# Sharing the tail chunk of two batches' keys, and making all 1601st keys in one product

## The chip, the core and the metric

The kernel runs on one core of a Trainium2 chip. Times are device microseconds of one launch. TensorE is called PE here (PEld its weight loads), VectorE DVE, ScalarE ACT, GpSimd POOL; SP is the queue that issues nearly all transfers.

## What is computed

A small transformer of three layers runs on x, of 16 batches x 64 rows x 256. What matters here is the first layer's cross-attention: each batch has its own context of 1601 rows x 256. From it come 8 heads of 128 keys each, every key is layer-normalised over its 128 numbers, and two query heads attend to each key head. Cut to that:

```python
kvx = jnp.einsum('bsi,oi->bso', cond, w_kv_x)          # cond: (16, 1601, 256)
kx, vx = jnp.split(kvx, 2, axis=-1)
kx = _ln(kx.reshape(b, sc, g, d), kxln_w, kxln_b)      # g = 8 heads, d = 128
xout = _gqa(qx, kx, vx).reshape(b, s, nh * d)          # softmax(qx kx / sqrt(d)) vx
```

Self-attention with 8-bit weights stands beside it in that layer, and its output and xout are rounded and projected together. A block attention with a feed-forward and a second feed-forward follow; they touch the change only by sharing the engines.

## The kernel before

**Tiles.** The 16 batches are taken two at a time, which gives 8 tiles (index i) of 128 query rows. The 8 key heads are taken in two halves of 4 (index hh)[...]. A batch (bb, 0 or 1 within its tile) and a half make a *unit*, and the two units of one tile and half make a *pair*; there are 32 units and 16 pairs. The 1601 keys of a unit are cut into NC = 13 chunks, 12 of 128 and a last one, the tail, of 65 (`TAIL`).

**One chunk's way**, all in `unit`:
- `load_T` (L471) fetches two chunks of the transposed context at once into `ctxT` (4 buffers); the tail is fetched alone, as 65 columns;
- `project` (L484) multiplies by the half's key weights `wkx`: two matmuls (L488) into one of two PSUM buffers of the pool `ps_mm`; ACT squares the result (L493). The weights have their mean over each head taken out beforehand by `centre`, so that normalising needs the squares only;
- `squares` (L496): DVE sums the squares per head (L499), POOL makes the inverse root in `rsqrt` (L159, L160);
- `normalise` (L504): DVE multiplies (L507), which frees the PSUM buffer;
- `transpose_k` (L517): PE transposes the four heads (L521), ACT applies the normalisation's weight and bias while copying out (L523), giving `kT`;
- `score` (L529): PE multiplies keys and queries (L534), ACT copies the scores to a tile P of the pool `pp` (L539), and DVE keeps a running maximum (L544);
- `exponent` (L583): once the unit's maximum is known, DVE subtracts it (L585) and ACT takes the exponential (L589);
- `accumulate` (L591): PE multiplies P and the plain context `ctxN` (L604) into three PSUM banks, over all chunks of the unit.

After the tail the sums are divided, transposed, and in `pair_out` (L655) multiplied with the value weights for both batches of the pair.

**Order.** Nothing loops at run time. `at(step, rank, fn)` and `spawn(step, rank, generator)` put work into a heap, and `run` emits it by step, then by rank. A unit's chunk c is projected in step base + c, scored in base + c + 2, exponentiated in base + c + 18 and accumulated in base + c + 20; its context is asked for in base + c - 5. The units' bases are 13 steps apart, so each step carries one chunk of each of these stages, 416 steps in all, with the other layers' work spread between them. The layer below then lays out each engine's instruction stream in nearly this order; two calls of `behind` hold back some DVE instructions. A tile of a pool is given to a new user when all the readers of its former user are done. `pp` has 19 buffers of 512 columns.

```python
at(base + c, 2, lambda c=c: project(c))
at(base + c, 4.2, lambda c=c: squares(c))
at(base + c + 1, 1, lambda c=c: normalise(c))
at(base + c + 1, 6, lambda c=c: transpose_k(c))
at(base + c + 2, 5, lambda c=c: score(c))
```

The first half of `wkx` is loaded at the very start and centred in step -6, the second is loaded in step 6 and centred at the end of step 9. `more_constants` asks for the constants that are needed later, in step -1, all on SP's queue.

Of the kernel before, what the change touches and what calls it, by code (L numbers as in the profile page):

```python
# [14 lines left out]
F32 = mybir.dt.float32  # L15
# [3 lines left out]
AF = mybir.ActivationFunctionType  # L19
ALU = mybir.AluOpType  # L20
AX = mybir.AxisListType
PSUM = bass.MemoryType.PSUM

P = 128
B, S, H = 16, 64, 256
T = 1601
NH, G, D = 16, 8, 128
NT = B * S // P
NP = 4
NC = (T + P - 1) // P  # L30
TAIL = T - (NC - 1) * P
EPS = 1e-5
FP8_MAX = 448.0
INTER = 704
# [24 lines left out]
def body(tc, ctx, a):  # L59
    nc = tc.nc  # L60
    V, A, PE, GP = nc.vector, nc.scalar, nc.tensor, nc.gpsimd

    const = ctx.enter_context(tc.tile_pool(name="const", bufs=1))
    small = ctx.enter_context(tc.tile_pool(name="small", bufs=8))
    wp = ctx.enter_context(tc.tile_pool(name="wp", bufs=10))
    ctxp = ctx.enter_context(tc.tile_pool(name="ctxp", bufs=4))
    kp = ctx.enter_context(tc.tile_pool(name="kp", bufs=3))
    pp = ctx.enter_context(tc.tile_pool(name="pp", bufs=19))
    qp = ctx.enter_context(tc.tile_pool(name="qp", bufs=2))
    one = ctx.enter_context(tc.tile_pool(name="one", bufs=1))  # L70
    dram = ctx.enter_context(tc.tile_pool(name="dram", bufs=2, space=bass.MemoryType.DRAM))
    ps_mm = ctx.enter_context(tc.tile_pool(name="ps_mm", bufs=2, space=PSUM))
# [3 lines left out]
    def tr_tile(name, dt=F32):  # L76
        return ps_s.tile([P, 512], dt, tag="s", name=name)

    def s_tile(name):
        return ps_s.tile([P, 512], F32, tag="s", name=name)  # L80
# [4 lines left out]
    def spawn(step, rank, gen):  # L85
        heapq.heappush(heap, (step, rank, next(count), gen))

    def at(step, rank, fn):
        def once():
            fn()  # L90
            yield 1

        spawn(step, rank, once())
# [16 lines left out]
    wkx = const.tile([P, 2, 1024], F32, tag="wkx", name="wkx")  # L110

    def col(name, j=0):
        s = _COLS[name].start + j
        return vec[:, s : s + 1]

    ident = const.tile([P, P], F32, tag="ident", name="ident")
# [28 lines left out]
    def more_constants():  # L145
        for i in range(1, NT):
            nc.sync.dma_start(out=xr[i], in_=xs_in[i])
        nc.sync.dma_start(out=rows, in_=a["rows"].partition_broadcast(P))
        nc.sync.dma_start(out=shp, in_=a["shapes"])


    def rsqrt(out, in_, scale, g):

        n = in_.shape[0]
        ve = small.tile([P, 8], F32, tag="ve", name="ve")
        if scale is None:
            GP.tensor_scalar(ve[:n, :g], in_, EPS, None, ALU.add)
        else:
            GP.tensor_scalar(ve[:n, :g], in_, scale, EPS, ALU.mult, ALU.add)  # L159
        GP.tensor_tensor(out, ve[:n, :g], nhalf[:n, :g], ALU.pow)  # L160
# [49 lines left out]
    def v2(t):  # L210
        return t.rearrange("p (k o) -> p k o", k=2)
# [109 lines left out]
    def project(out, xq, ws, o, n):  # L321
        for k in range(2):
            for e, w in enumerate(ws):
                PE.matmul(  # L324
                    out, lhsT=xq[:, k, :], rhs=v2(w)[:, k, o : o + n],
                    start=k + e == 0, stop=k == 1 and e == len(ws) - 1,
                )
# [125 lines left out]
    def rows_of(c):  # L453
        return P if c < NC - 1 else TAIL

    pairs, mark = {}, {}

    def behind(ins, other):

        tc.add_manual_dep(  # L460
            ins.ins, other.ins.name,
            mybir.DependencyInfo(mybir.DependencyClass.NoSync, mybir.DependencyReason.DATA), reason="order",
        )

    def unit(i, hh, bb, base):
        b = 2 * i + bb
        last = b == B - 1 and hh == 1
        st = {"cxT": {}, "cxN": {}, "ps": {}, "ss": {}, "rs": {}, "kn": {}, "kT": {}, "P": {}, "pT": {}}
        pair = pairs.setdefault((i, hh), {})

        def load_T(c):  # L471
            t0 = c * P
            n = min(256, T - t0)
            t = ctxp.tile([P, 2, 256], F32, tag="ctxT", name="ctxT")
            nc.sync.dma_start(out=t[:, :, :n], in_=a["ctx"][b].rearrange("(k p) t -> p k t", p=P)[:, :, t0 : t0 + n])
            st["cxT"][c // 2] = t

        def load_N(c):
            n = rows_of(c)
            t = next(ctxn_next)  # L480
            nc.sync.dma_start(out=t[:n, 0:H], in_=a["ctx_n"][b][c * P : c * P + n, :])
            st["cxN"][c] = t

        def project(c):  # L484
            n, o = rows_of(c), (c % 2) * P
            ps = ps_mm.tile([P, 512], F32, tag="mm", name="ps_k")
            for k in range(2):
                PE.matmul(  # L488
                    ps[:n, :], lhsT=st["cxT"][c // 2][:, k, o : o + n], rhs=wkx[:, k, 512 * hh : 512 * (hh + 1)],
                    start=k == 0, stop=k == 1,  # L490
                )
            sq = one.tile([P, 512], F32, tag="sq", name="sq")
            A.activation(sq[:n], ps[:n], AF.Square)  # L493
            st["ps"][c], st["ss"][c] = ps, sq

        def squares(c):  # L496
            n = rows_of(c)
            ss = small.tile([P, 4], F32, tag="ss", name="ss")
            mark["ss"] = V.reduce_sum(ss[:n], st["ss"].pop(c)[:n].rearrange("p (g d) -> p g d", g=4), axis=AX.X)  # L499
            rs = small.tile([P, 4], F32, tag="rsx", name="rsx")  # L500
            rsqrt(rs[:n], ss[:n], 1.0 / D, 4)
            st["rs"][c] = rs

        def normalise(c):  # L504
            n, ps, rs = rows_of(c), st["ps"].pop(c), st["rs"].pop(c)
            kn = one.tile([P, 512], F32, tag="kn", name="kn", bufs=2)
            mark["kn"] = V.tensor_tensor(  # L507
                kn[:n].rearrange("p (g d) -> p g d", g=4), ps[:n].rearrange("p (g d) -> p g d", g=4),
                rs[:n].unsqueeze(2).to_broadcast([n, 4, D]), ALU.mult,
            )  # L510

            for name in ("M", "mx"):
                if name in mark:
                    behind(mark["kn"], mark[name])
            st["kn"][c] = kn

        def transpose_k(c):  # L517
            n, kn = rows_of(c), st["kn"].pop(c)
            tr = tr_tile("tr_kx")
            for g in range(4):  # L520
                PE.transpose(tr[:, g * P : g * P + n], kn[:n, g * D : (g + 1) * D], ident[:n, :n])  # L521
            kT = kp.tile([P, 4, P], F32, tag="kT", name="kT")
            A.activation(  # L523
                kT[:, :, 0:n], tr.rearrange("p (g t) -> p g t", g=4)[:, :, 0:n],
                AF.Identity, bias=col("kxln_b"), scale=col("kxln_w"),
            )
            st["kT"][c] = kT

        def score(c):  # L529

            n, kT = rows_of(c), st["kT"].pop(c)
            ps = s_tile("s")
            for g in range(4):
                PE.matmul(  # L534
                    ps[:n, g * P : (g + 1) * P], lhsT=kT[:, g, 0:n],
                    rhs=qxs[i, hh][:, bb, 2 * g : 2 * g + 2, :].rearrange("p h s -> p (h s)"), start=True, stop=True,
                )
            pc = pp.tile([P, 512], F32, tag="P", name="P")
            A.activation(pc[:n], ps[:n], AF.Copy, scale=C_ATT)  # L539
            if c == 0:  # L540
                st["M"] = one.tile([P, 512], F32, tag="M", name="M")
                mark["M"] = V.tensor_copy(st["M"], ps)
            else:
                mark["M"] = V.tensor_tensor(st["M"][:n], ps[:n], st["M"][:n], ALU.max)  # L544
            st["P"][c] = pc
# [82 lines left out]
            A.copy(pair["pc"][:, k, :, bb, :], tr.rearrange("p (g q) -> p g q", g=4))  # L628

        for c in range(NC):  # L630
            if c % 2 == 0:
                at(base + c - 5, 0, lambda c=c: load_T(c))
            at(base + c, 2, lambda c=c: project(c))
            at(base + c, 4.2, lambda c=c: squares(c))
            at(base + c + 1, 1, lambda c=c: normalise(c))
            at(base + c + 1, 6, lambda c=c: transpose_k(c))
            at(base + c + 2, 5, lambda c=c: score(c))
            at(base + c + 17, 0, lambda c=c: load_N(c))
            at(base + c + 18, 8, lambda c=c: exponent(c))
            at(base + c + 20, 3.5, lambda c=c: accumulate(c))  # L640
# [401 lines left out]
    at(6, 0, lambda: load_wkx(1))  # L1042
    at(9, 9, lambda: centre(1))
    at(-1, 0, more_constants)
    EX = 4.0
    for i in range(NT):
        base = 52 * i
# [6 lines left out]
        )  # L1054
        spawn(ln0, EX, ln_tile(i))
        for p in range(4):
            spawn(sa0[p] - 2, EX, self_attention(i, p))
            spawn(qx0[p] - 2, EX, queries(i, p))
        l0 = base + {NT - 3: 96, NT - 2: 80, NT - 1: 74}.get(i, 92)
# [79 lines left out]
```

## Time and profile before

| | us |
|---|---|
| median of 3 runs | 2729.69 |
| lowest, highest | 2727.47, 2730.16 |
| the profiled execution's own time | 2729.8 |
| its span, first to last instruction | 2728.0 |
| busy: PE, PEld | 2616.5, 2022.0 |
| busy: DVE, ACT, POOL | 1892.1, 1410.4, 847.3 |

The mean granted PE clock was 0.985. The profile is of one execution. A group of instructions is one line of the kernel, one engine, one shape; in a timeline its columns are start, length, engine, line, operation, output and inputs, and in square brackets the idle time before it with what ended it. For matmuls the first pair of numbers (128*65) is the stationary operand, 65 being the number of keys, and what follows (128x512) the streamed one. Every fp32 matmul of the program shows as two instructions, so that a chunk's product, two matmuls, is a group of x4; a transpose is one.

### The profile page before, as it was taken

What the parts mean: (1) busy time and instruction counts of PE and PEld (TensorE: products, weight loads), DVE (VectorE), ACT (ScalarE), POOL (GpSimd) and SP (SyncE); (2) the same over time, 40 slices, a digit from 0 to 9 for tenths busy, and PEclk for the clock granted to TensorE, in tenths of its full rate; (3) what the DMA queues carried; (4) which work ended last, traced back from release to release, by engine and by line L of the source; (5) the groups of instructions that cost most, each with busy time, mean ns of one, the idle gap of its engine ahead of it and who ended that gap; (6) DMA issues with size and microseconds to landing.
All of it is one profiled execution on the core that took longest, in us unless ns stands there. A gap on an engine that the chain in (4) does not pass through costs nothing.

```text
span 2728.0 us, 41628 instructions
## 1 busy us (share of the span) xinstructions
PE 2616.5 (96%) x14835; PEld 2022.0 (74%) x14835; DVE 1892.1 (69%) x4637; ACT 1410.4 (52%) x2572; POOL 847.3 (31%) x1248
## 2 busy tenths in 40 slices
PE   6999989999999999999999999999999999999996
PEld 4677767778777787777877777777777777777784
DVE  7877766767666676677766676776767767666654
ACT  4555545445565455645457445564555644545431
POOL 3433333333333323333233333323333233333200
PEclk9999999999999999999999999999999999999997
DMA  7655634333344323433334343443434334342131
GB/s 257 198 172 195 236 126 136 115 97 123 111 149 143 115 88 119 152 126 123 107 118 136 122 128 111 132 139 99 140 109 134 124 106 130 108 145 82 47 106 39
DMA packets 213735, 350.91 MB, mean 129 GB/s; under 512 B 27068, under 2 KB 154264, under 8 KB 213528
## 3 DMA queue, kind: packets, MB, share of 16 engines
q1 hardware_dynamic: 213240, 348.09, 40.0%
q8 instruction: 117, 1.92, 0.3%
q14 instruction: 90, 0.74, 0.1%
q10 hardware_dynamic: 288, 0.17, 0.0%
HBM read 325.31 MB, written 22.87 MB: 128 GB/s over the span
## 4 chain that ended last, share of the span: by engine, by line
PE 71%; DVE 17%; POOL 6%; ACT 4%; issue 2%; DMA 1%; SPq 0%; ACTq 0%; POOLq 0%; DVEq 0%
PE ps_k L488 21%; PE acc L604 20%; PE s L534 10%; PE tr_kx L521 5%; DVE ss L499 2%; POOL rs L160 2%; PE po_p L278 2%; DVE P L585 2%; DVE M L544 2%; DVE kn L507 2%; PE po_x L669 2%; POOL rsx L160 1%; PE ps_q L324 1%; POOL ve L159 1%; DVE st L168 1%
## 5 line engine op out<-in xcount | busy, mean ns | idle before, releaser
L604 PEld LDWEIGHTS acc<-ctxN,P 128*128 128x128 f32 (+1 forms) x4160 | 709.5, 191 | 178.1 <-issue 108.7
L488 PE MATMUL ps_k<-wkx,ctxT 128*128 128x512 f32 (+1 forms) x1664 | 802.0, 602 | 7.2 <-DVE wkx L1035 6.8
L604 PE MATMUL acc<-ctxN,P 128*128 128x257 f32 (+5 forms) x4160 | 801.5, 340 | 0.0
L159 POOL TENSOR_SCALAR ve<-ss 128x4 f32<-128x4 f32 (+2 forms) x432 | 213.5, 494 | 1455.5 <-DVE ss L499 1375.9
L589 ACT ACTIVATE P<-P 128x512 f32<-128x512 f32 (+1 forms) x416 | 261.2, 630 | 526.8 <-DVE P L585 525.9
L534 PE MATMUL s<-qx,kT 128*128 128x128 f32 (+1 forms) x3328 | 444.7, 276 | 18.5 <-ACT kT L523 7.7
L160 POOL TENSOR_TENSOR rsx<-ve,nhalf 128x4 f32<-128x4 f32 (+1 forms) x416 | 439.7, 1057 | 31.7
L488 PEld LDWEIGHTS ps_k<-wkx,ctxT 128*128 128x128 f32 (+1 forms) x1664 | 284.3, 190 | 207.2 <-issue 196.1
L534 PEld LDWEIGHTS s<-qx,kT 128*128 128x128 f32 (+1 forms) x3328 | 405.6, 187 | 38.3 <-ACT kT L523 12.5
L544 DVE TENSOR_TENSOR M<-s,M 128x512 f32<-128x512 f32 (+1 forms) x384 | 263.7, 687 | 235.4 <-ACT P L539 233.2
L493 ACT ACTIVATE sq<-ps_k 128x512 f32<-128x512 f32 (+1 forms) x416 | 248.4, 597 | 339.0 <-PE ps_k L488 333.0
L499 DVE TENSOR_REDUCE ss<-sq 128x4 f32<-128x512 f32 (+1 forms) x416 | 283.3, 681 | 137.2 <-ACT sq L493 135.3
L523 ACT ACTIVATE kT<-tr_kx,vec 128x512 f32<-128x512 f32 (+1 forms) x416 | 315.9, 759 | 30.8 <-PE tr_kx L521 30.6
L539 ACT ACTIVATE P<-s 128x512 f32<-128x512 f32 (+1 forms) x416 | 246.9, 593 | 156.9 <-PE s L534 154.4
L507 DVE TENSOR_TENSOR kn<-ps_k,rsx 128x512 f32<-128x512 f32 (+1 forms) x416 | 283.0, 681 | 15.5 <-POOL rsx L160 15.2
L585 DVE TENSOR_TENSOR P<-P,mx 128x512 f32<-128x512 f32 (+1 forms) x416 | 282.2, 681 | 0.0
L521 PE MATMUL tr_kx<-ident,kn 128*128 128x128 f32 (+1 forms) x1664 | 247.5, 272 | 25.7 <-DVE kn L507 14.8
L521 PEld LDWEIGHTS tr_kx<-ident,kn 128*128 128x128 f32 (+1 forms) x1664 | 192.9, 143 | 38.7 <-DVE kn L507 12.7
L178 DVE TENSOR_SCALAR qn<-qn,mv,rs 128x128 f32<-128x128 f32 x256 | 77.2, 345 | 85.3 <-POOL rs L172 85.2
L160 POOL TENSOR_TENSOR rs<-ve,nhalf 128x4 f32<-128x4 f32 (+2 forms) x144 | 113.8, 790 | 8.3
L168 DVE BATCH_NORM_STATS2 st<-qn 128x6 f32<-128x128 f32 x256 | 63.7, 272 | 40.0 <-ACT qn L334 40.0
L159 POOL TENSOR_SCALAR ve<-mv,wsq 128x4 f32<-128x4 f32 (+1 forms) x96 | 28.8, 300 | 186.6 <-DVE mv L169 177.6
(200 smaller groups left out, 2633.8 us busy)
## 6 DMA issues: line engine op xcount, KB each, us to landing
wproj<-wproj SPq DMA_DIRECT2D x120, 512.0 KB
ctxT<-in_ctx SPq DMA_DIRECT2D x192, 256.0 KB
ctxN<-in_ctx_n SPq DMA_DIRECT2D x384, 128.0 KB
wq<-wq SPq DMA_DIRECT2D x56, 512.0 KB
wkv<-wkv SPq DMA_DIRECT2D x56, 512.0 KB
wqx<-wqx SPq DMA_DIRECT2D x56, 512.0 KB
wvx<-in_w_kv_x SPq DMA_DIRECT2D x16, 512.0 KB
wup<-in_ffn_up_w SPq DMA_DIRECT2D x16, 512.0 KB
```

Of the source, the lines that this page charges most:

```text
L159: GP.tensor_scalar(ve[:n, :g], in_, scale, EPS, ALU.mult, ALU.add)
L160: GP.tensor_tensor(out, ve[:n, :g], nhalf[:n, :g], ALU.pow)
L488: PE.matmul(ps[:n, :], lhsT=st["cxT"][c // 2][:, k, o : o + n], rhs=wkx[:, k, 512 * hh : 512 * (hh + 1)], start=k == 0, stop=k == 1,)
L499: mark["ss"] = V.reduce_sum(ss[:n], st["ss"].pop(c)[:n].rearrange("p (g d) -> p g d", g=4), axis=AX.X)
L507: mark["kn"] = V.tensor_tensor(kn[:n].rearrange("p (g d) -> p g d", g=4), ps[:n].rearrange("p (g d) -> p g d", g=4), rs[:n].unsqueeze(2).t ...
L521: PE.transpose(tr[:, g * P : g * P + n], kn[:n, g * D : (g + 1) * D], ident[:n, :n])
L523: A.activation(kT[:, :, 0:n], tr.rearrange("p (g t) -> p g t", g=4)[:, :, 0:n], AF.Identity, bias=col("kxln_b"), scale=col("kxln_w"),)
L534: PE.matmul(ps[:n, g * P : (g + 1) * P], lhsT=kT[:, g, 0:n], rhs=qxs[i, hh][:, bb, 2 * g : 2 * g + 2, :].rearrange("p h s -> p (h s)"), st ...
L544: mark["M"] = V.tensor_tensor(st["M"][:n], ps[:n], st["M"][:n], ALU.max)
L585: ins = V.tensor_tensor(pc[:n], pc[:n], st["mx"][:n].rearrange("p g q -> p (g q)"), ALU.subtract)
L589: A.activation(pc[:n], pc[:n], AF.Exp)
L604: PE.matmul(ps, lhsT=pc[:n, g * P : (g + 1) * P], rhs=cx[:n, o : o + w], start=g == 2 and c == 0, stop=c == NC - 1 and (g, o) in ((2, 0), ...
```

## The change

The tail of 65 keys is taken apart into 64 and 1 (`REST` = 64).

- The 64 last whole keys of the two batches of a pair are put side by side: `load_T` of the first batch's tail fetches both as two transfers into one `ctxT` tile, and this chunk of 128 keys goes through product, squares, normalisation and transposes once per pair, in the first batch's steps. The second batch's tail has none of these steps any more.
- The result goes to a tile `kT_tail` of one buffer, [128, 4 heads, 2 batches, 65]. ACT writes 64 of each 65 columns, and POOL copies the 65th from `k_last` (8 numbers per partition). Each batch's score of its tail reads its own 65 columns of `kT_tail`.
- `k_last` holds the 1601st keys of all 16 batches, made once per half by `last_keys`: a product of 16 rows, its squares, normalisation, four transposes of 16 keys and ACT's copy. It is emitted in steps 3.6 to 4.8 and 15.6 to 16.8. The 1601st context rows come from a new input, transposed, [256, 16], in one transfer at the end of `more_constants`.
- `pp` has 18 buffers in place of 19.
- `project`, `squares` and `normalise` call the new functions `square`, `roots` and `normalised`, which hold their former lines.

The diff, cut to its core:

```diff
 NP = 4
 NC = (T + P - 1) // P
 TAIL = T - (NC - 1) * P
+REST = TAIL - 1
 EPS = 1e-5
 FP8_MAX = 448.0
 INTER = 704
...
     wp = ctx.enter_context(tc.tile_pool(name="wp", bufs=10))
     ctxp = ctx.enter_context(tc.tile_pool(name="ctxp", bufs=4))
     kp = ctx.enter_context(tc.tile_pool(name="kp", bufs=3))
-    pp = ctx.enter_context(tc.tile_pool(name="pp", bufs=19))
+    pp = ctx.enter_context(tc.tile_pool(name="pp", bufs=18))
     qp = ctx.enter_context(tc.tile_pool(name="qp", bufs=2))
     one = ctx.enter_context(tc.tile_pool(name="one", bufs=1))
     dram = ctx.enter_context(tc.tile_pool(name="dram", bufs=2, space=bass.MemoryType.DRAM))
...
             nc.sync.dma_start(out=xr[i], in_=xs_in[i])
         nc.sync.dma_start(out=rows, in_=a["rows"].partition_broadcast(P))
         nc.sync.dma_start(out=shp, in_=a["shapes"])
+        nc.sync.dma_start(out=ctx_last, in_=a["ctx_last"].rearrange("(k p) b -> p k b", p=P))
+
+
+    ctx_last = const.tile([P, 2, B], F32, tag="ctx_last", name="ctx_last")
+    k_last = const.tile([P, 2, 4, B], F32, tag="k_last", name="k_last")
 
 
     def rsqrt(out, in_, scale, g):
...
             mybir.DependencyInfo(mybir.DependencyClass.NoSync, mybir.DependencyReason.DATA), reason="order",
         )
 
+    def square(ps, n):
+        sq = one.tile([P, 512], F32, tag="sq", name="sq")
+        A.activation(sq[:n], ps[:n], AF.Square)
+        return sq
+
+    def roots(sq, n):
+        ss = small.tile([P, 4], F32, tag="ss", name="ss")
+        mark["ss"] = V.reduce_sum(ss[:n], sq[:n].rearrange("p (g d) -> p g d", g=4), axis=AX.X)
+        rs = small.tile([P, 4], F32, tag="rsx", name="rsx")
+        rsqrt(rs[:n], ss[:n], 1.0 / D, 4)
+        return rs
+
+    def normalised(ps, rs, n):
+        kn = one.tile([P, 512], F32, tag="kn", name="kn", bufs=2)
+        mark["kn"] = V.tensor_tensor(
+            kn[:n].rearrange("p (g d) -> p g d", g=4), ps[:n].rearrange("p (g d) -> p g d", g=4),
+            rs[:n].unsqueeze(2).to_broadcast([n, 4, D]), ALU.mult,
+        )
+        return kn
+
+    def last_keys(hh):
+        ps = ps_mm.tile([P, 512], F32, tag="mm", name="ps_k")
+        for k in range(2):
+            PE.matmul(
+                ps[:B, :], lhsT=ctx_last[:, k, :], rhs=wkx[:, k, 512 * hh : 512 * (hh + 1)], start=k == 0, stop=k == 1
+            )
+        sq = square(ps, B)
+        yield 0.4
+        rs = roots(sq, B)
+        yield 0.4
+        kn = normalised(ps, rs, B)
+        yield 0.4
+        tr = tr_tile("tr_kx")
+        for g in range(4):
+            PE.transpose(tr[:, g * P : g * P + B], kn[:B, g * D : (g + 1) * D], ident[:B, :B])
+        A.activation(
+            k_last[:, hh], tr.rearrange("p (g t) -> p g t", g=4)[:, :, 0:B],
+            AF.Identity, bias=col("kxln_b"), scale=col("kxln_w"),
+        )
+
     def unit(i, hh, bb, base):
         b = 2 * i + bb
         last = b == B - 1 and hh == 1
...
 
         def load_T(c):
             t0 = c * P
-            n = min(256, T - t0)
             t = ctxp.tile([P, 2, 256], F32, tag="ctxT", name="ctxT")
-            nc.sync.dma_start(out=t[:, :, :n], in_=a["ctx"][b].rearrange("(k p) t -> p k t", p=P)[:, :, t0 : t0 + n])
+
+            for j, n in [(0, 256)] if c < NC - 1 else [(0, REST), (1, REST)]:
+                nc.sync.dma_start(
+                    out=t[:, :, j * n : (j + 1) * n],
+                    in_=a["ctx"][b + j].rearrange("(k p) t -> p k t", p=P)[:, :, t0 : t0 + n],
+                )
             st["cxT"][c // 2] = t
 
         def load_N(c):
...
             st["cxN"][c] = t
 
         def project(c):
-            n, o = rows_of(c), (c % 2) * P
+            n, o = P, (c % 2) * P
             ps = ps_mm.tile([P, 512], F32, tag="mm", name="ps_k")
             for k in range(2):
                 PE.matmul(
                     ps[:n, :], lhsT=st["cxT"][c // 2][:, k, o : o + n], rhs=wkx[:, k, 512 * hh : 512 * (hh + 1)],
                     start=k == 0, stop=k == 1,
                 )
-            sq = one.tile([P, 512], F32, tag="sq", name="sq")
-            A.activation(sq[:n], ps[:n], AF.Square)
-            st["ps"][c], st["ss"][c] = ps, sq
+            st["ps"][c], st["ss"][c] = ps, square(ps, n)
 
         def squares(c):
-            n = rows_of(c)
-            ss = small.tile([P, 4], F32, tag="ss", name="ss")
-            mark["ss"] = V.reduce_sum(ss[:n], st["ss"].pop(c)[:n].rearrange("p (g d) -> p g d", g=4), axis=AX.X)
-            rs = small.tile([P, 4], F32, tag="rsx", name="rsx")
-            rsqrt(rs[:n], ss[:n], 1.0 / D, 4)
-            st["rs"][c] = rs
+            st["rs"][c] = roots(st["ss"].pop(c), P)
 
         def normalise(c):
-            n, ps, rs = rows_of(c), st["ps"].pop(c), st["rs"].pop(c)
-            kn = one.tile([P, 512], F32, tag="kn", name="kn", bufs=2)
-            mark["kn"] = V.tensor_tensor(
-                kn[:n].rearrange("p (g d) -> p g d", g=4), ps[:n].rearrange("p (g d) -> p g d", g=4),
-                rs[:n].unsqueeze(2).to_broadcast([n, 4, D]), ALU.mult,
-            )
+            kn = normalised(st["ps"].pop(c), st["rs"].pop(c), P)
 
             for name in ("M", "mx"):
                 if name in mark:
...
             st["kn"][c] = kn
 
         def transpose_k(c):
-            n, kn = rows_of(c), st["kn"].pop(c)
+            kn = st["kn"].pop(c)
             tr = tr_tile("tr_kx")
             for g in range(4):
-                PE.transpose(tr[:, g * P : g * P + n], kn[:n, g * D : (g + 1) * D], ident[:n, :n])
-            kT = kp.tile([P, 4, P], F32, tag="kT", name="kT")
-            A.activation(
-                kT[:, :, 0:n], tr.rearrange("p (g t) -> p g t", g=4)[:, :, 0:n],
-                AF.Identity, bias=col("kxln_b"), scale=col("kxln_w"),
-            )
-            st["kT"][c] = kT
+                PE.transpose(tr[:, g * P : (g + 1) * P], kn[:, g * D : (g + 1) * D], ident)
+            if c < NC - 1:
+                kT = st["kT"][c] = kp.tile([P, 4, P], F32, tag="kT", name="kT")
+                out, src = kT, tr.rearrange("p (g t) -> p g t", g=4)
+            else:
+                kT = pair["kT"] = one.tile([P, 4, 2, TAIL], F32, tag="kT_tail", name="kT_tail")
+                GP.tensor_copy(kT[:, :, :, REST], k_last[:, hh, :, b : b + 2])
+                out, src = kT[:, :, :, 0:REST], tr.rearrange("p (g e t) -> p g e t", g=4, e=2)
+            A.activation(out, src, AF.Identity, bias=col("kxln_b"), scale=col("kxln_w"))
 
         def score(c):
 
-            n, kT = rows_of(c), st["kT"].pop(c)
+            n, kT = rows_of(c), st["kT"].pop(c) if c < NC - 1 else pair["kT"][:, :, bb, :]
             ps = s_tile("s")
             for g in range(4):
                 PE.matmul(
...
             A.copy(pair["pc"][:, k, :, bb, :], tr.rearrange("p (g q) -> p g q", g=4))
 
         for c in range(NC):
-            if c % 2 == 0:
-                at(base + c - 5, 0, lambda c=c: load_T(c))
-            at(base + c, 2, lambda c=c: project(c))
-            at(base + c, 4.2, lambda c=c: squares(c))
-            at(base + c + 1, 1, lambda c=c: normalise(c))
-            at(base + c + 1, 6, lambda c=c: transpose_k(c))
+            if c < NC - 1 or bb == 0:
+                if c % 2 == 0:
+                    at(base + c - 5, 0, lambda c=c: load_T(c))
+                at(base + c, 2, lambda c=c: project(c))
+                at(base + c, 4.2, lambda c=c: squares(c))
+                at(base + c + 1, 1, lambda c=c: normalise(c))
+                at(base + c + 1, 6, lambda c=c: transpose_k(c))
             at(base + c + 2, 5, lambda c=c: score(c))
             at(base + c + 17, 0, lambda c=c: load_N(c))
             at(base + c + 18, 8, lambda c=c: exponent(c))
...
     at(6, 0, lambda: load_wkx(1))
     at(9, 9, lambda: centre(1))
     at(-1, 0, more_constants)
+    for hh in range(2):
+        spawn(3.6 + 12 * hh, 2.2, last_keys(hh))
     EX = 4.0
     for i in range(NT):
         base = 52 * i
...
+        "ctx_last": t(n["ctx_2048"][:, T - 1, :]),
```

## The prediction

> **What bounds the kernel now.** I read the page's busy line first, then its chain of waits, then one pair of batches in the timeline, TensorE (PE) alone and then ScalarE (ACT) alone, with busy times by stretch.
>
> ```profile
> PE 2616.5 (96%) x14835; PEld 2022.0 (74%) x14835; DVE 1892.1 (69%) x4637; ACT 1410.4 (52%) x2572; POOL 847.3 (31%) x1248
> PE 71%; DVE 17%; POOL 6%; ACT 4%; issue 2%; DMA 1%; SPq 0%; ACTq 0%; POOLq 0%; DVEq 0%
> ```
>
> PE has 96% of the span and the chain names PE for 71% of it. But the ends of matmuls are modelled, so I price PE by the distance from one group's start to the next one's start, not by durations.
>
> ```profile
> 957.28 0.60 PE L521 MATMUL tr_kx<-ident,kn 128*128 128x128 f32 x4
> 957.72 1.88 PE L488 MATMUL ps_k<-wkx,ctxT 128*65 128x512 f32 x4
> 959.43 1.91 PE L604 MATMUL acc<-ctxN,P 128*128 128x257 f32 x10
> 961.18 0.60 PE L342 MATMUL tr_q<-ident,qn 128*128 128x128 f32 x4
> 961.61 1.06 PE L534 MATMUL s<-qx,kT 128*128 128x128 f32 x8
> 962.51 0.60 PE L521 MATMUL tr_kx<-ident,kn 128*128 128x128 f32 x4
> 962.94 1.88 PE L488 MATMUL ps_k<-wkx,ctxT 128*128 128x512 f32 x4
> 964.66 0.60 PE L869 MATMUL tr_p<-ident,sm 128*128 128x128 f32 x4
> ...
> 967.96 0.41 PE L521 MATMUL tr_kx<-ident,kn 65*128 65x65 f32 x4
> 968.21 1.99 PE L669 MATMUL po_x<-pc,wvx 128*128 128x256 f32 x8
> ```
>
> This is a second batch's tail chunk (second batch of a pair). Its product with 65 keys takes 957.72 to 959.43 = 1.71 us; a full chunk's, with 128 keys, 962.94 to 964.66 = 1.72. Four transposes of 128 keys take 957.28 to 957.72 = 0.44, of 65 keys 967.96 to 968.21 = 0.25. The groups follow each other without a hole: PE is fed here and sets the pace. The stretches say how near the others are:
>
> ```profile
> 957.70:962.90 5.20, 5.20 (x32) 3.92 (x31) 3.73 (x6) 3.71 (x7) 0.77 (x3) 1.00 0.29 76
> 970.00:977.40 7.40, 7.40 (x51) 6.26 (x51) 6.92 (x18) 0.79 (x2) 1.37 (x2) 1.00 0.38 119
> 1122.30:1128.40 6.10, 6.10 (x40) 4.83 (x39) 2.92 (x5) 5.73 (x9) 1.78 (x3) 1.00 0.52 149
> ```
>
> The columns are length, then busy PE, weight load, DVE, ACT, POOL. PE is full in each; ACT has 3.71 of 5.20 in the first, and in other steps DVE (6.92 of 7.40) or ACT (5.73 of 6.10) is nearly full too.
>
> [...]65 keys are as dear as 128 (1.71 against 1.72 us), as both stream 512 columns; and a transpose, which streams one column per key, falls from 0.44 to 0.25. [...]the group of 1.88 us is followed after 1.71. [...]
>
> **The change, part by part.** Two batches and one half of the heads make a pair; there are 8 x 2 = 16.
>
> Removed and put back on PE: a pair now has two tail chunks, 2 x (1.715 + 0.25) = 3.93 us; it will have one of 128 keys, 1.715 + 0.44 = 2.155. Saved 1.775, times 16 = 28.4 us. Scores (L534) and accumulation (L604) keep their 65 rows. With a tail chunk go also, off PE, one Square (L493, 0.593 us), one sum (L499, 0.676), POOL's two steps (0.576 and 1.031), one normalisation (L507, 0.677); and two kT of 128x260 (0.575 each) become one of 128x512 (0.775). All of this lies beside PE: I count nothing.
>
> Added: the 1601st keys, twice. On PE each is 1.715 plus four transposes of 16 keys, at least 0 and at most the 0.25 of 65: 3.9 us for both with the upper end. They run in steps 3.6 and 15.6, before accumulation begins. The product takes one of the two PSUM buffers, so the next product waits until the previous chunk is normalised: Square 0.60, sum 0.68, POOL 0.50 + 1.06, normalisation 0.68 = 3.52 us after its product, while PE has score 0.90 + transposes 0.44 + the new product 1.72 = 3.06. That is 0.5 us of waiting, and again for the buffer that the new product holds: about 1.0 each, 2.0 for both. Bounds: 0 (PE had such holes there anyway, 38.65 waits 0.90 us for kn) and 7.0 (both chains bare).
>
> ACT's lag. Taking the product away brings PE to the next score 1.71 us earlier, and that score needs kT of the chunk before. In the pair shown, ACT makes it late:
>
> ```profile
> 957.70 0.63 ACT L589 ACTIVATE P<-P 128x512 f32<-128x512 f32 x1 [3.54 <-DVE P L585]
> 958.24 0.76 ACT L343 ACTIVATE qx<-tr_q,vec 128x512 f32<-128x512 f32 x1
> 959.09 0.63 ACT L865 ACTIVATE sm<-sm 128x512 f32<-128x512 f32 x1
> 959.62 0.58 ACT L539 ACTIVATE P<-s 128x512 f32<-128x512 f32 x1
> 960.10 0.77 ACT L523 ACTIVATE kT<-tr_kx,vec 128x512 f32<-128x512 f32 x1
> ```
>
> PE would want its score at 961.61 - 1.71 = 959.90; kT is ready at 960.87, so PE waits 1.0 us. ACT runs without a hole from 957.70, begun by DVE's subtraction, which the change doesn't touch, and the built order keeps these five. Reading the same place in all 16 pairs, kT is this late in the second pair of batch tiles 1 to 5; in the others it is ready over 1.7 us before its score. So 5 x 1.0 = 5.0 us come back. Bounds: 0, and 16 x 1.0 = 16 if ACT or DVE catches PE in every pair (rivals).
>
> The copy of two 1601st keys into the shared chunk is one POOL instruction per pair, 128x8; the nearest row is L159 at 0.50 us for 128x4. Behind it on POOL is the next chunk's rsqrt, and ACT's tail activation waits for it, with that chunk's Square and PE's score queued after. I take nothing: POOL is busy 31%, and its only old user is the preceding pair's last score, some 12 steps back. Without that cover: 16 x 0.5 = 8 us. No reason lets it gain.
>
> Loads: 32 loads of 65 columns become 32 of 64, two in a row, five steps ahead of use; one small load (ctx_last) stands in SP's queue behind the constants and before two context loads. SP issues one in 0.3 to 0.5 us, with DMA at 40%: nothing. If landing were late, only the first product would wait.
>
> The pool of score tiles goes from 19 to 18. A tile lives from its score to its accumulation. In the built order at most 17 older ones are unaccumulated when a score is issued, before and after, so 18 suffice: nothing. A smaller pool cannot gain.
>
> Sum against the profiled execution, 2729.8 us (span 2728.0 and 1.8 around it): 28.4 - 3.9 - 2.0 - 5.0 = 17.5, so 2712.3. The median of the runs, 2729.69, is the same to 0.1, so no shift.
>
> **Rivals.** (B) Everything comes through: ACT catches up elsewhere and the product's waits fall into existing holes. 28.4 - 3.9 = 24.5, giving 2705.3. For it: PE's digit is 9 in 37 of the 40 slices of the page, so PE sets the pace; against: the five late kT. (C) The vacated time is refilled in every pair, ACT or DVE being next by 1.0 us: 28.4 - 5.9 - 16 = 6.5, giving 2723.3. For it: 6.92 of 7.40 and 5.73 of 6.10 above; against: both engines lose about 1 us of work at the same place. (D) Slower: the pool of 18. If tiles come free later than the order suggests, ACT's score copy (L539) waits for an accumulation, 959.43 to 961.18 = 1.75 us. Over 416 chunks a mean wait of 17.5 / 416 = 0.042 us cancels the gain; one chunk in 20 (21 x 1.75 = 36.8 us) gives 2749.1. For it: 19 were held before; against: PE accumulates just before it scores, and the copy comes after both. (E) The gain is eaten at the start: the instruction order there is rearranged, and PE already waits up to 5.8 us for kn near 373 us (the longest of 11 such waits); two of 6 would leave 5.5 us, 2724.3. That the change removes nothing is excluded: the built list has no 65-wide product any more.
>
> **How the numbers follow.** Forecast (2712.3, give or take 4) 0.55, B 0.20, C 0.17, D 0.05, E 0.03. About 0.2%, 5.5 us, is what a measurement can tell from no change, so faster is under 2724.2: forecast, B and 0.10 of C, 0.85; within: 0.07 of C and E, 0.10; slower: D, 0.05. A range from 2703 to 2723 holds the forecast, B and half of C, 0.83.
>
> **What would show it.** In the changed profile: L488's successor with 16 fewer tail groups and no 65-wide form; per pair about 1.8 us less from one pair's first product to the next pair's; PE waiting about 1 us for ACT's kT at five tails; two products from ctx_last costing 3 us each; no wait of ACT for POOL at the shared tail. I am wrong if the tails' holes are much longer than 1 us or elsewhere, or if ACT's score copies wait for PE's accumulation.

## The result and the profile after

| | before | after |
|---|---|---|
| median, us | 2729.96 (7 runs) | 2718.46 (7 runs) |
| lowest, highest | 2727.47, 2732.08 | 2715.51, 2725.53 |
| profiled execution's own time | 2729.8 | 2716.17 |
| its span | 2728.0 | 2714.1 |
| mean granted PE clock | 0.985 | 0.983 |

The ratio is 0.9961, with an interval of 0.9949 to 0.9973. The kernel became 11.5 us faster by the medians; the forecast was 17.4 us, 2712.3. So the measured median lies inside the stated range of 2703 to 2723, but outside the forecast's own 2708 to 2716. A second set of six runs of the kernel after gave 2720.2.

The busy line and the first line of the chain, from the page of the kernel after, and its group of products:

```profile
PE 2596.3 (96%) x14715; PEld 2014.8 (74%) x14723; DVE 1873.2 (69%) x4609; ACT 1398.8 (52%) x2544; POOL 825.3 (30%) x1236
PE 67%; DVE 20%; POOL 7%; ACT 4%; issue 2%; DMA 1%; ACTq 0%; SPq 0%; POOLq 0%; DVEq 0%
L538 PE MATMUL ps_k<-wkx,ctxT 128*128 128x512 f32 x1600 | 775.5, 605 | 6.0 <-DVE wkx L1076 5.5
```

PE is still busy 96% of the span; the product has one form, 1600 matmuls, and the 128 of 65 keys are gone. The chain gives PE 4 points less and DVE 3 more: more of the path runs through other engines, for which PE waits. Now the place that the forecast priced, the second tail of a pair, PE first:

```profile
957.46 1.91 PE L644 MATMUL acc<-ctxN,P 128*128 128x257 f32 x10
959.20 0.60 PE L348 MATMUL tr_q<-ident,qn 128*128 128x128 f32 x4
960.67 1.16 PE L574 MATMUL s<-qx,kT 128*128 128x128 f32 x8 [0.87 <-ACT kT L567]
961.67 0.60 PE L559 MATMUL tr_kx<-ident,kn 128*128 128x128 f32 x4
```

Between transposes and accumulation there is no product any more, and PE stands 0.87 us until ACT's kT is there. ACT in the same stretch:

```profile
957.45 0.63 ACT L629 ACTIVATE P<-P 128x512 f32<-128x512 f32 x1 [3.55 <-DVE P L625]
957.99 0.76 ACT L349 ACTIVATE qx<-tr_q,vec 128x512 f32<-128x512 f32 x1
958.84 0.63 ACT L906 ACTIVATE sm<-sm 128x512 f32<-128x512 f32 x1
959.37 0.58 ACT L579 ACTIVATE P<-s 128x512 f32<-128x512 f32 x1
959.85 0.77 ACT L567 ACTIVATE kT<-tr_kx,vec 128x512 f32<-128x512 f32 x1
```

These are the five instructions of before, in the same order and begun by the same subtraction.

**Where the time went.** I took every PE matmul's distance to the next one's start. The usual distance of its kind (line and shape) is "spacing"; of what lies above it, the part at an idle time of PE over 0.1 us is "waits", and otherwise the part in which the granted clock was low is "half clock". In us:

| | before | after | difference | forecast |
|---|---|---|---|---|
| spacing | 2509.2 | 2485.0 | -24.3 | -24.5 |
| waits | 123.8 | 129.9 | +6.0 | +7.0 |
| half clock | 28.5 | 32.3 | +3.8 | 0 |
| the rest | 60.9 | 61.4 | +0.5 | 0 |
| sum | | | -14.0 | -17.5 |

So the two terms that the forecast had are right to 1 us as sums, and a term that it did not have, the clock, took 3.8 back. Cut by place, the first 104 scored chunks (tiles 0 and 1) end later than before, at 654.3 us against 651.9: spacing -3.1, waits +2.3, half clock +2.3, rest +0.9. All the gain comes from chunk 104 on: 16.4 us. Of the 3.8 us of half clock, too, 2.3 belong to the first 104 chunks.

The two traces differ by 14.0 us, the medians by 11.5: runs of the kernel after differ among themselves by up to 10 us. A trace of its second set (e5_after_again, 2721.6 us) has the same spacing as the first, 8.8 us more waits than before and 7.4 us more half clock.

**The half clock.** The tile's costliest wait is in both kernels PE's transpose of the maximum (L551 before, L591 after), for ACT's qx. Before, PE alone, then by stretch; the stretches end with PEclk, DMA share and GB/s:

```profile
1223.96 1.16 PE L534 MATMUL s<-qx,kT 128*128 128x128 f32 x8 [0.26 <-DVE M L544]
1227.61 1.11 PE L551 MATMUL tr_m<-ident,M 128*128 128x128 f32 x4 [2.49 <-ACT qx L343]
1228.52 3.08 PE L488 MATMUL ps_k<-wkx,ctxT 128*128 128x512 f32 x4
```

```profile
1224.10:1227.50 3.40, 1.02 (x8) 0.82 (x8) 2.59 (x7) 1.24 (x3) 1.58 (x2) 1.00 0.00 1
...
1227.50:1230.90 3.40, 3.29 (x7) 1.91 (x8) 2.14 (x6) 1.73 (x10) 0.00 (x0) 0.50 0.00 0
1231.00:1241.00 10.00, 10.00 (x61) 7.90 (x60) 5.13 (x10) 5.53 (x10) 3.14 (x4) 1.00 0.25 79
```

In 3.40 us PE works 1.02; the next 3.40 us run at a clock of 0.50, and the product behind the wait takes 3.08 us where it took 1.88. After, the same place:

```profile
1220.70:1224.10 3.40, 1.41 (x11) 1.08 (x9) 3.25 (x8) 0.59 (x2) 1.05 (x2) 1.00 0.12 37
1224.10:1227.50 3.40, 2.64 (x7) 1.61 (x8) 1.49 (x5) 2.38 (x11) 0.53 (x1) 0.50 0.00 0
1227.50:1230.90 3.40, 3.40 (x10) 2.06 (x9) 1.73 (x4) 1.14 (x3) 0.01 (x1) 0.50 0.12 21
```

Two stretches of 3.40 run at half clock. At this wait in five tiles, before had 3.4, 6.8, 3.4, 6.8, 3.4 us of half clock, after 3.4, 3.4, 6.8, 6.8, 6.8. The starts before (568.7, 896.4, 1227.5, 1555.2, 1886.3 us) lie 327.7, 331.1, 327.7 and 331.1 us apart, 96.0, 97.0, 96.0 and 97.0 times 3.413. The 3.413 us are an estimate from the two traces: all stretches of low clock, 14 in before and 16 in after, begin within 0.03 us of one such grid in each, and those that end inside the span last 3.41 us or two to four times that. In the 3.40 us before the half clock PE was not idle, it still worked 1.02, 30%; a wait of 2.49 us was enough.

### The profile page after: what moved, and what is told of

Its sections match the earlier page's. It is cut to its first block, busy times and chain, and to the rows that moved or that the text cites. A ratio compares the mean times of both kernels' runs of the same rounds, so it can differ in the third digit from the quotient of the medians.

```text
span 2714.1 us, 41389 instructions
## 1 busy us (share of the span) xinstructions
PE 2596.3 (96%) x14715; PEld 2014.8 (74%) x14723; DVE 1873.2 (69%) x4609; ACT 1398.8 (52%) x2544; POOL 825.3 (30%) x1236
## 4 chain that ended last, share of the span: by engine, by line
PE 67%; DVE 20%; POOL 7%; ACT 4%; issue 2%; DMA 1%; ACTq 0%; SPq 0%; POOLq 0%; DVEq 0%
PE ps_k L538 19%; PE acc L644 19%; PE s L574 10%; PE tr_kx L559 5%; POOL rs L166 3%; DVE ss L478 3%; DVE kn L485 2%; DVE M L584 2%; DVE P L625 2%; PE po_p L284 2%; POOL rsx L166 2%; POOL ve L165 2%; DVE st L174 2%; DVE qn L184 2%; PE po_x L710 1%
## 5 line engine op out<-in xcount | busy, mean ns | idle before, releaser
L538 PE MATMUL ps_k<-wkx,ctxT 128*128 128x512 f32 x1600 | 775.5, 605 | 6.0 <-DVE wkx L1076 5.5
L166 POOL TENSOR_TENSOR rsx<-ve,nhalf 128x4 f32<-128x4 f32 x402 | 421.2, 1048 | 30.5
L574 PE MATMUL s<-qx,kT 128*128 128x128 f32 x3072 | 411.5, 277 | 15.5 <-DVE hd L1014 4.8
L538 PEld LDWEIGHTS ps_k<-wkx,ctxT 128*128 128x128 f32 x1600 | 278.9, 194 | 197.6 <-issue 187.7
L473 ACT ACTIVATE sq<-ps_k 128x512 f32<-128x512 f32 x402 | 240.2, 597 | 341.1 <-PE ps_k L538 331.9
L574 PEld LDWEIGHTS s<-qx,kT 128*128 128x128 f32 x3072 | 378.1, 192 | 33.1 <-ACT kT L567 7.6
L478 DVE TENSOR_REDUCE ss<-sq 128x4 f32<-128x512 f32 x402 | 273.7, 681 | 142.2 <-ACT sq L473 140.7
L579 ACT ACTIVATE P<-s 128x512 f32<-128x512 f32 (+1 forms) x416 | 246.3, 592 | 144.4 <-PE s L574 142.8
L567 ACT ACTIVATE kT<-tr_kx,vec 128x512 f32<-128x512 f32 x384 | 297.3, 774 | 31.4 <-PE tr_kx L559 31.1
L485 DVE TENSOR_TENSOR kn<-ps_k,rsx 128x512 f32<-128x512 f32 x402 | 273.5, 681 | 17.8 <-POOL rsx L166 17.7
L559 PE MATMUL tr_kx<-ident,kn 128*128 128x128 f32 x1600 | 245.0, 276 | 26.7 <-DVE kn L485 14.1
L165 POOL TENSOR_SCALAR ve<-mv,wsq 128x4 f32<-128x4 f32 (+1 forms) x96 | 29.8, 311 | 189.6 <-DVE mv L175 181.9
```

Of the source, the lines that this page charges most:

```text
L478: mark["ss"] = V.reduce_sum(ss[:n], sq[:n].rearrange("p (g d) -> p g d", g=4), axis=AX.X)
L485: mark["kn"] = V.tensor_tensor(kn[:n].rearrange("p (g d) -> p g d", g=4), ps[:n].rearrange("p (g d) -> p g d", g=4), rs[:n].unsqueeze(2).t ...
L538: PE.matmul(ps[:n, :], lhsT=st["cxT"][c // 2][:, k, o : o + n], rhs=wkx[:, k, 512 * hh : 512 * (hh + 1)], start=k == 0, stop=k == 1,)
L559: PE.transpose(tr[:, g * P : (g + 1) * P], kn[:, g * D : (g + 1) * D], ident)
L567: A.activation(out, src, AF.Identity, bias=col("kxln_b"), scale=col("kxln_w"))
L574: PE.matmul(ps[:n, g * P : (g + 1) * P], lhsT=kT[:, g, 0:n], rhs=qxs[i, hh][:, bb, 2 * g : 2 * g + 2, :].rearrange("p h s -> p (h s)"), st ...
```

## The experiments

Ratios are to the kernel before, medians in us. The kernel before had 2730.5 beside runs e1 to e4 and again beside e9 to e11, and 2731.5 beside e5 to e8.

**The pool alone** (e1_pool18, in the kernel before):

```diff
-pp = ctx.enter_context(tc.tile_pool(name="pp", bufs=19))
+pp = ctx.enter_context(tc.tile_pool(name="pp", bufs=18))
```

> The kernel before with 18 score tiles in place of 19, nothing else. My theory (a tile is free before the score that takes it over, so 18 cost nothing): within 3 us of the kernel before, and ACT's score copies wait for PE no more than there (154 us in all). The rival that part of the change's missing gain goes to the smaller pool: 4 to 6 us slower than before.

Measured: 2731.9 (2727.6 to 2734.9), ratio 1.0004 (0.9996 to 1.0012). ACT's score copies wait 152.7 us for PE, against 154.4 before (and 142.8 in the kernel after). The smaller pool costs nothing; rival D is out.

**Without the 1601st keys** (e2_no_last, in the kernel after; they are zeros in `k_last`, so this part of the computation is left out):

```diff
-    for hh in range(2):
-        spawn(3.6 + 12 * hh, 2.2, last_keys(hh))
+    GP.memset(k_last, 0.0)
```

> The changed kernel without the product of the 1601st keys; k_last is set to zero, so the 1601st keys are left out. My theory: the two products cost 5.9 us as I reckoned (3.9 on PE, 2.0 of waiting), so 2712 to 2713 against 2718.5 for the changed kernel. The rival that the start alone ate the missing gain: 8 to 10 us, 2709. The rival that they fall into holes that PE has there anyway: under 3 us, 2716 or more.

Measured: 2715.8 (2711.6 to 2717.8), ratio 0.9942 (0.9929 to 0.9954), 2.7 below the kernel after, in ranges that overlap. In the trace the spacing up to chunk 26 falls from 125.2 to 121.2: the two products and their transposes cost the 4.0 us that the forecast gave them (3.9). Its 2.0 us of waits for PSUM are not there: the waits in that stretch are 29.8 without the new products and 29.1 with them. The 4.0 does not come out whole, since waits and half clock between chunks 52 and 104 grew by 2.1 and 2.8, in a part that the edit does not touch. That is the run's chance: the second trace of the kernel after (e5_after_again) has as much there without the edit.

**The five late kT on DVE** (e3_kt_dve, in the kernel after):

```diff
+            if (hh, bb, c) == (1, 1, 10) and 1 <= i <= 5:
+                V.tensor_scalar(out, src, col("kxln_w"), col("kxln_b"), ALU.mult, ALU.add)
+                return
```

> The changed kernel, but at the five tails where the trace shows PE waiting 1.03 us for ACT's kT, DVE writes that one kT in place of ACT. My theory (ACT's own queue makes it late, DVE has a hole of over 1 us there): PE's five waits go, 5 us less, 2713 to 2714. The rival that DVE is just as full there: DVE hands the 0.7 us on to the normalisation and the time stays at 2717 to 2720, or rises.

Measured: 2712.5 (2711.1 to 2715.6), ratio 0.9936 (0.9923 to 0.9948), 6 us below the kernel after. That looks like the theory, but the trace says otherwise. PE at the place shown above:

```profile
961.26 1.06 PE L577 MATMUL s<-qx,kT 128*128 128x128 f32 x8
962.95 0.65 PE L559 MATMUL tr_kx<-ident,kn 128*128 128x128 f32 x4 [0.63 <-DVE kn L485]
```

The score no longer waits, but the transposes behind it do, for DVE's normalisation: DVE now does the kT first. Per middle tile, waits stay at 9.5 us, and the half clock falls from 3.0 to between 0 and 1.7. So the five waits come back on DVE, and what was gained is clock.

**The copy on DVE** (e4_copy_dve, in the kernel after). The profile after shows POOL held up by the copy of the 1601st keys; its length (ns: least, median, most), then what POOL waited for before it (us, times):

```profile
L565 POOL COPY kT_tail<-k_last x16: 191/197/201, 47.7 to 2445.3; 128x8 f32<-128x8 f32 x16
...
PE s L574: 45.3, 8
```

```diff
-                GP.tensor_copy(kT[:, :, :, REST], k_last[:, hh, :, b : b + 2])
+                V.tensor_copy(kT[:, :, :, REST], k_last[:, hh, :, b : b + 2])
```

> The changed kernel with the copy of the 1601st keys on DVE in place of POOL. In the trace POOL stands up to 8.9 us before this copy with its queue held. My theory (nothing on POOL is needed in that time): 0 to 2 us of difference to 2718.5, and none of it a gain of PE. The rival that POOL's held queue delays the inverse roots and so PE: 3 to 5 us less, 2714.

Measured: 2719.2 (2715.3 to 2720.3), ratio 0.9955 (0.9943 to 0.9967): no difference. POOL's 45 us of standing delay nobody.

**The kernel after again** (e5_after_again), for the next three, which share its chip:

> The changed kernel itself once more, on one chip with the next three. Theory and rivals: 2715 to 2722, 8 to 15 us below the kernel before; a spread that goes with the granted clock, about 4 us for each thousandth less.

Measured: 2720.2 (2716.2 to 2726.9), ratio 0.9963 (0.9949 to 0.9977). In its profile all five tiles have 6.8 us of half clock, and the half clock costs 35.9 us in all, 7.4 more than before. The times go with the clock, but not by 4 us: from 2716.2 at 0.985 to 2726.9 at 0.981, 2.7 us for each thousandth.

**The query step earlier, in both kernels** (e6_qx_early after, e8_before_qx before), to take the long wait itself away; it concerns tiles 2 to 7:

```diff
-            base - 23, [base + o for o in (-16, -4, 8, 22)], [base + o for o in (-14, -5, 12, 20)]
+            base - 23, [base + o for o in (-16, -4, 8, 22)], [base + o for o in (-15, -5, 12, 20)]
```

> The changed kernel with the first of a tile's four query products for the cross-attention one step earlier (tiles 2 to 7). In the trace PE waits 2.65 us in each of five tiles for the PSUM buffer that ACT frees with the copy of these queries, and just then the clock is granted at half for 3.4 or 6.8 us. My theory: the wait brings the half clock, so both go: 5 x 2.65 = 13 of waiting and 5 x 1.7 to 3.4 = 8 to 17 of clock, 2690 to 2700. The rival that the half clock comes by time and not by the wait: only the 13 go, about 2705, and the half windows stay in the middle tiles. The rival that the wait only moves to the next user of a PSUM buffer: 2716 to 2720.

> The kernel before with the query product one step earlier, without the change. My theory: the wait of 2.65 us and the half clock after it are the same in it, so it gains the same 20 to 28 us, 2702 to 2710, and the difference to the changed kernel with the same edit, now free of the clock's chance, is 17.5 to 19 us (24.3 of spacing less 6 of waits). The rival that the missing gain of the change is not the clock's: the difference stays at 11 to 14 us.

Measured: e6 2691.3 (2689.1 to 2692.1), ratio 0.9853 (0.9840 to 0.9865); e8 2705.2 (2702.8 to 2706.3), ratio 0.9903 (0.9891 to 0.9916). PE of e6 at the place, and its stretches:

```profile
1211.43 1.04 PE L574 MATMUL s<-qx,kT_tail 128*65 128x128 f32 x8
1213.10 0.66 PE L559 MATMUL tr_kx<-ident,kn 128*128 128x128 f32 x4 [0.63 <-ACT qx L349]
```

```profile
1200.00:1212.00 12.00, 12.00 (x75) 9.71 (x74) 8.28 (x18) 6.00 (x12) 5.93 (x11) 1.00 0.36 114
1212.20:1219.00 6.80, 6.17 (x39) 4.81 (x38) 5.07 (x14) 3.37 (x7) 2.25 (x4) 1.00 0.07 22
```

The wait for qx shrinks from 2.49 to 0.63 us and the clock stays at 1.00. A middle tile takes 321.5 us in e6 (327.7 after) and 324.0 in e8 (328.8 or 330.0 before). With no half clock in the middle tiles of either, the change is worth 324.0 - 321.5 = 2.5 us per tile: 3.6 of spacing less one late kT, 1.1, as forecast. But the distance of the medians, 13.9 us, is not the 17.5 I looked for. In these two traces the loss sits between chunks 52 and 104: 322.0 us in e6 and 318.7 in e8, though the spacing there is 3.6 less. One trace of each says little about this stretch: the two traces of the kernel after take 323.5 and 328.3 us there, and e7 below, with the same work as e6 there, 318.0.

**Both edits** (e7_qx_kt, in the kernel after):

> The changed kernel with both edits, kT on DVE at five tails and the query product one step earlier. My theory: the gains add, 5 us below the run with the early query product alone, 2685 to 2695. Rivals: if DVE is as full as ACT there, no difference to that run.

Measured: 2688.8 (2683.3 to 2691.4), ratio 0.9842 (0.9829 to 0.9855): 2.5 below e6 in ranges that overlap, so the kT on DVE adds little once the clock is held.

**The sums over partitions on PE** (e9_qx_ones after, e10_before_qx_ones before, with the earlier query step in both). Between chunks 52 and 104 the ternary weights' means are made with three all-reduces on POOL. POOL of e6 around one, and PE at the same time:

```profile
341.33 1.01 POOL L166 TENSOR_TENSOR rsx<-ve,nhalf 128x4 f32<-128x4 f32 x1
348.59 0.40 POOL L766 PARTITION_ALL_REDUCE tot<-asum  x1 [6.25 <-DVE M L584]
356.53 0.35 POOL L165 TENSOR_SCALAR ve<-ss 128x4 f32<-128x4 f32 x2 [7.54 <-issue]
```

```profile
352.73 1.91 PE L644 MATMUL acc<-ctxN,P 65*128 65x257 f32 x10
358.68 1.11 PE L559 MATMUL tr_kx<-ident,kn 128*128 128x128 f32 x4 [4.04 <-DVE kn L485]
```

The operation takes 0.40 us, but POOL does nothing else from 342.3 to 356.5. Late row sums are not the reason: DVE has finished them at 341.3. In the traces of before, after, e6 and e8 POOL stands 5.7 to 6.4 us before each of the three and 6.7 to 8.7 us behind it. The inverse roots that the keys need wait behind it; PE stands 4.04 us and goes on at a lower clock (0.63 from 358.8 to 365.0 us).

```diff
+    ones = const.tile([P, 1], F32, tag="ones", name="ones")
+    GP.memset(ones, 1.0)
...
-            tot = small.tile([P, 1], F32, tag="tot", name="tot")
-            GP.partition_all_reduce(tot, asum[:, 0:1], P, bass_isa.ReduceOp.add)
             yield 1
+            tot = s_tile("tot")[:, 0:1]
+            PE.matmul(tot, lhsT=ones[:, 0:1].to_broadcast([P, P]), rhs=asum[:, 0:1], start=True, stop=True)
```

> The kernel after, with the query step one step earlier (as in e6_qx_early, 2691.3 us) and the three sums over partitions in the ternary weights' means made by TensorE (a product of a column of ones, read as 128x128, with the 128 row sums) instead of GpSimd's all-reduce. The sums are the same up to rounding. Theory (the gain that is still missing between e8 and e6, 13.9 us of some 18 expected, went into the three waits of TensorE around the all-reduce, 13.5 us in e6 against 9.7 in e8, and into the half clock that follows them): those waits fall below 1 us each, no half clock between 340 and 400 us, so 2691.3 - 12 to -17 = 2674 to 2679, and the distance to e10 grows from 13.9 to 17 to 19 us. Rival (the start lost it through its rearranged order, somewhere else in the first two tiles): faster too, but by no more than e10 is against e8, and the distance stays at 14 us. Rival 2 (the new products wait for DVE's row sums and hold one of the three score buffers): no gain or slower than 2691.

> The same two edits in the kernel before (with 18 score buffers, which cost nothing in e1_pool18), for the distance to e9. Its all-reduce waits were 9.7 us in e8_before_qx (2705.2 us). Theory: 2705.2 - 8 to -11 = 2694 to 2697; e9 stands 17 to 19 us below it. Rival: the distance stays at 14 us, as e8 to e6.

Measured: e9 2672.5 (2670.4 to 2673.0), ratio 0.9788 (0.9774 to 0.9801); e10 2690.4 (2690.0 to 2693.4), ratio 0.9857 (0.9844 to 0.9871). e6 first, then e9, by stretch:

```profile
335.00:360.00 25.00, 20.43 (x118) 15.91 (x117) 18.88 (x41) 9.05 (x17) 4.62 (x8) 0.93 0.41 123
360.00:385.00 25.00, 20.04 (x101) 14.63 (x100) 11.16 (x31) 9.48 (x17) 6.68 (x12) 0.91 0.43 136
385.00:410.00 25.00, 20.95 (x97) 14.64 (x96) 16.39 (x41) 11.78 (x26) 6.57 (x12) 0.89 0.29 96
```

```profile
335.00:360.00 25.00, 24.78 (x144) 18.82 (x143) 17.14 (x45) 12.48 (x23) 7.85 (x11) 1.00 0.22 58
360.00:385.00 25.00, 24.51 (x147) 19.58 (x146) 16.20 (x43) 13.37 (x25) 10.52 (x16) 1.00 0.17 49
385.00:410.00 25.00, 25.00 (x142) 19.02 (x142) 20.91 (x42) 13.47 (x30) 7.97 (x11) 1.00 0.39 118
```

PE's busy time in these 75 us goes from 61.42 to 74.29 and the clock is 1.00 throughout. The stretch from chunk 52 to 104 is now 303.9 us in e9 and 307.6 in e10: 3.7 less, its spacing's worth, where e6 stood 3.2 above e8. And the distance of the medians goes from 13.9 to 17.9, the theory's 17 to 19. Taking the extremes of the runs, it was 10.7 to 17.1 and is 17.0 to 23.0; the traces give 3.7 against -3.2. Counted as in the table above, e9 has 24.1 us less spacing than e10, 7.8 us more waits and 1.3 us less half clock, close to the forecast's -24.5, +7.0 and 0.

The edit moves the work as well as the engine: the products run at 384.6 to 434.2 us in e9, the all-reduces at 348.6 to 391.1 in e6. That the waits came from the all-reduces rests on POOL's standing in the traces; later all-reduces were not tried.

**All edits together** (e11_qx_kt_ones):

> All edits that were found to help: the kernel after, query step one step earlier, the five late kT on DVE, and the sums over partitions on TensorE. e7_qx_kt had 2688.8 us. Theory: as much below it as e9 is below e6, 12 to 17 us: 2672 to 2677. Rival (the five kT on DVE and the earlier step share a gain): e9's time within 1 us.

Measured: 2671.5 (2668.8 to 2674.7), ratio 0.9788 (0.9774 to 0.9801), within 1 us of e9: the rival. e9's two edits are what helps; e9 is 46 us (1.7%) below the kernel after, and 58 below the kernel before.

## Why the prediction was right, and what it missed

**The saved spacing** (28.4 - 3.9 = 24.5): right, 24.3 in the profile, and 4.0 for the new products by e2. This is the mechanism that was forecast. By its time alone, 2718.5, the result is nearer to rival C's 2723.3 than to the forecast's 2712.3; it is the trace that tells them apart.

**The five late kT** (5.0): right in place and size. PE waits for kT near 633, 959, 1287, 1614 and 1942 us, 1.03 us of distance each. No other tail of a second batch got a new wait of this size, so rival C is out, and so is B, which had none of them. e3 shows that moving this kT to DVE only turns the wait over to DVE.

**The new product's waits for PSUM** (2.0): not found (e2). The two products cost 2.0 us each and not the 3 that the prediction looked for. Chunks 26 to 52 wait 2.4 us more (2.9 against 0.5), but e2, which has no such product, has the same 2.9, so these waits come from something else in the rearranged start; what it is was not tried.

**The longer kT of the shared tail**, which the sum put at nothing as lying beside PE. At eleven of the first batches' tails PE waited for ACT's kT already before. ACT now writes 128x512 there in 0.78 us, where it wrote 128x260 in 0.57; near 887 us PE's wait grows from 0.51 to 0.81 us. Over the eleven tails PE's distances grow by 2.0 us in all. So the sum of the waits came near (+6.0 for 7.0) partly by luck: one item of 2.0 was not there, and another of 2.0 was left out.

**Nothing for pool, copy and loads**: pool and copy confirmed by e1 and e4; the loads had no run of their own, but among PE's waits in the profile after none is for a transfer. The reason given for the copy was wrong: I took POOL's queue to find the old user long done, and it waited 45.3 us in eight places. It cost nothing because nothing behind it was due.

**The step that is missing** from the sum: I took the granted clock as given. Before, 28.5 us were already lost to half clock, and I read the mean of 0.985 without asking which waits made it. The change moved those waits against the clock's grid. From chunk 156 to 312 a tile now takes 327.65 to 327.69 us, which is 96.0 times 3.413, so that the wait falls at the same place of the grid in each tile and costs two stretches each time; before, 328.8 and 330.0 alternated, and so did one and two. That the length of the tile decides it was not shown: the length contains the tile's own half clock (the tile before these, with one stretch, took 326.4), so the two cannot be told apart here. These tiles also hold the smaller part of the 3.8 us; 2.3 lie before chunk 104. That the wait causes the half clock was shown: e6 and e8 shortened it from 2.49 to under 0.8 us and the half clock of the middle tiles went with it.

**Rival E** (eaten at the start) had the right place with too large a price. It named PE's waits for kn near 373 us and took 12 us; in the first two tiles the waits and the half clock grew by 2.3 each. In e9 and e10, with the all-reduces gone, that stretch gives its full gain, and the change is worth 17.9 us, close to the sum's 17.5. By this one comparison, what was lost there went into waits and clock around the all-reduces.

Open: how much of the first 26 chunks' +3.2 us (179.5 against 176.3) belongs to the change. In the three pairs (before and after, e8 and e6, e10 and e9) the kernel with it is slower there by 2.0 to 6.2 us, of which 2.1 is spacing. The rest varies from run to run: e1, which differs from the kernel before in the pool alone, has 178.2 there.

## What to carry to other kernels

Before pricing a change, list the waits of TensorE that are followed by a lower granted clock, and price each as the wait plus the half clock behind it (here 2.49 us, and 3.4 or 6.8 us at a clock of 0.50); a change that merely shifts them in time can lose part of its gain to them (here 3.8 of 17.5 us in one trace) or gain by them (e3). Take such waits away first: moving one small step one place earlier brought more here (26 us before, 29 after) than the change itself. And when an edit helps, look whether the wait that it aimed at has gone: in e3 it had only changed its name.

## What the runs showed of the hardware

A wait of TensorE of 2.49 us brought 3.4 or 6.8 us at a clock of 0.50, on a grid of 3.41 us. A wait of 0.63 us at the same place in e6 and one of 0.87 for ACT's kT in the kernel after brought none: the clock stayed at 1.00. Around an all-reduce over partitions, 0.40 us long, POOL stood 6.25 us before it and 7.54 behind it, and around each of the twelve in four traces much the same (5.7 to 6.4 us before, 6.7 to 8.7 behind). Replacing three of them by products, which ran later, saved 15 us (e8 to e10) to 19 us (e6 to e9); two matmuls with one streamed column, 0.21 us each, do one sum.
